# Turning denominators and normed tokens with DVE squares and DRAM transfers instead of TensorE transposes, in a two-layer attention kernel

## The chip, the cores and the metric

The kernel runs on one core of a Trainium2 chip, in 32-bit floating point. The metric is the device time of one execution in microseconds (us). Engine names are those of the profile: PE is TensorE's products, PEld its weight loads, DVE is VectorE, ACT is ScalarE, POOL is GpSimd, SP issues most transfers.

## The reference, cut to what matters

The input x has 4 batches of 128 channels and 4096 positions (64 x 64).

```python
# layer 0, per batch, with 64 inner channels m
q, k, v = wq @ xf, wk @ xf, wv @ xf                  # (64, 4096) each
att = softmax(k.T @ q, over j)                        # 4096 x 4096
x = x + wo @ (att @ v.T).T
# layer 1, on tokens t = x.T, 128 channels
t = t + causal_attention(layernorm(t), Wq, Wk, Wv)    # 4096 x 4096, scale 128 ** -0.5
# recurrent layer: Wx = layernorm(t) @ W.T, normalised over all tokens with gamma and beta
y_t = sigmoid(Wx_t + y_(t-1) @ V.T)
t = t + y
```

What must be seen for the change: both attentions end in a softmax whose denominators are sums over keys, and both are followed by a layernorm over the 128 channels of a token, whose result is used in two layouts, tokens on partitions and channels on partitions.

## The kernel before, in words

The fast path treats layer 0 of a batch, then layer 1 of the same batch, then the next batch; after the fourth batch comes the recurrent stage. Queries are taken in blocks g of 512 (8 per batch and layer). For each block the keys are passed in items; an item is a pair of key tiles of 128. In layer 0 a block has 16 items. Layer 1 is causal, so block g has 2g full items and two shorter ones on the diagonal: block 0 has 2 items, block 7 has 16.

One loop over all items, in slots, sets the order of the work. In slot s, `scores` (L656 in layer 0, L665 in layer 1) multiplies keys by the block's query rows into s_ps, and ACT takes the exponential into one of four buffers p (L670, L672). In layer 1 POOL clears what lies above the diagonal (L676). `sums` (L694 to L704) adds p into dsum on DVE. Two slots later `values` (L716, L724) multiplies p by the values and accumulates in acc. With the last item of a block, `values` copies acc out (L735 and L736, or L738) to agg, and DVE adds the two halves of dsum to den (L740), which has keys on partitions and the block's 512 queries along the row. The denominator of a query is therefore the sum of den over the partitions.

What follows a block is done in steps that are pushed into a list with a slot at which they fall due; at most one of them is taken per slot:

- `project` (L523 to L541): PE turns den in four 128x128 transposes into den_ps (L528), DVE sums each row of it (L530) and takes the reciprocal (L531). PE multiplies agg by the output weights into o_ps (L534), and DVE scales by the reciprocals and adds to xs, which holds the residual by tokens (L539).
- `normed` (L543 to L557): DVE takes mean and variance of each token (L548, L549), POOL the power -0.5 (L436), DVE one step of refinement (L437 to L440) and the normed tokens xh (L555).
- `transposed` (L559 to L564): PE turns the four 128x128 tiles of xh into a PSUM tile, and ACT (layer 0, xhT_ps) or DVE (layer 1, xh2T_ps) copies it to xhT.

In layer 0 (`finish0`) projection and norm fall due two slots after the block's last values; the transposes wait in the list `fill` for the end of the next block. In layer 1 (`finish1`) there are three steps, 1, 3 and 1 slots apart: projection, norm and the store of the tokens to x2 in DRAM; the transposes; the product with W into wx_ps (L609), its statistics (L612), and a copy to xs that reorders columns by time step (L614).

`rows` prepares the query rows of the block after the next. In layer 1 it is a product with xhT (L519) and a copy on DVE (L521); in layer 0 it also issues the load of the tokens of in_xT over xs (L512), on SP's queue. While layer 1 of a batch runs, `side` holds the key and value products of the next batch (L476, L488, L498), whose swapped halves go through transfers (L482), on SP's queue too.

The framework (Tile) decides the final order of instructions within each engine, close to but not exactly the order of the program. The pools: `misc` PSUM tiles have two buffers for all of den_ps, o_ps, r_ps, wx_ps, kr_ps and v_ps; the work pool has two buffers per name.

Of the kernel before, what the change touches and what calls it, by code (L numbers as in the profile page):

```python
# [9 lines left out]
F32 = mybir.dt.float32  # L10
AF = mybir.ActivationFunctionType
ALU = mybir.AluOpType
AX = mybir.AxisListType
PSUM = bass.MemoryType.PSUM

P = 128
BLK = 512
# [332 lines left out]
def fast_path(  # L350
# [21 lines left out]
    nc = tc.nc  # L372
    B, C, N = x.shape
    M = c_wqT.shape[1]
    assert C == P and M == P // 2 and N % CHUNK == 0
    NT = N // P
    NB = N // BLK
    TPB = BLK // P
    SHIFT = 32.0
    LOW, HIGH = 1e-25, 1e25  # L380
    WARM, TOL, STEPS = 12, 1e-6, 16
    NCH = N // STEPS
    CPB = BLK // STEPS

    const = ctx.enter_context(tc.tile_pool(name="const", bufs=1))
    xpool = ctx.enter_context(tc.tile_pool(name="x", bufs=1))
    dram = ctx.enter_context(tc.tile_pool(name="dram", bufs=1, space=bass.MemoryType.DRAM))

    xs = xpool.tile([P, B, N], F32, name="xs")
# [27 lines left out]
    ident = const.tile([P, P], F32, name="ident")  # L419
# [6 lines left out]
    nc.gpsimd.memset(mhalf, -0.5)  # L426
    minus = const.tile([P, P], F32, name="minus")
    nc.vector.tensor_scalar(minus, ident, -1.0, None, ALU.mult)
    good = const.tile([P, 1], F32, name="good")
    g1 = const.tile([P, P], F32, name="g1")  # L430
    recs = const.tile([P, 2, B, NT], F32, name="recs")
# [10 lines left out]
    with tc.tile_pool(name="batch", bufs=1) as batch, tc.tile_pool(name="rows", bufs=2) as rowp, tc.tile_pool(  # L442
        name="prob", bufs=4
    ) as prob, tc.tile_pool(name="work", bufs=2) as wk, tc.tile_pool(name="stat", bufs=4) as stat, tc.tile_pool(
        name="ps_s", bufs=2, space=PSUM
    ) as ps_s, tc.tile_pool(name="ps_a", bufs=1, space=PSUM) as ps_a, tc.tile_pool(
        name="ps_m", bufs=2, space=PSUM
    ) as ps_m:

        def misc(name):  # L450
            return ps_m.tile([P, BLK], F32, tag="m", name=name)
# [8 lines left out]
        bs = [Batch() for _ in range(B)]  # L460
# [60 lines left out]
            nc.vector.tensor_copy(r, ps)  # L521
            bs[b].next.append(r)

        def project(layer, b, g, agg, den):

            dp = misc("den_ps")
            for j in range(TPB):
                nc.tensor.transpose(dp[:, ts(j, P)], den[:, ts(j, P)], ident)  # L528
            rec = recs[:, layer, b, ts(g, TPB)]
            nc.vector.tensor_reduce(rec, dp.rearrange("p (j k) -> p j k", k=P), AX.X, ALU.add)  # L530
            nc.vector.reciprocal(rec, rec)  # L531
            op = misc("o_ps")
            for j in range(TPB):
                nc.tensor.matmul(  # L534
                    op[:, ts(j, P)], lhsT=agg[:, ts(j, P)], rhs=wv1 if layer else wo2, start=True, stop=True
                )
            for j in range(TPB):
                t = xs[:, b, ds(g * BLK + j * P, P)]
                nc.vector.scalar_tensor_tensor(  # L539
                    t, in0=op[:, ts(j, P)], scalar=rec[:, j : j + 1], in1=t, op0=ALU.mult, op1=ALU.add  # L540
                )  # L541

        def normed(b, g, dst):  # L543

            st = stat.tile([P, TPB, nc.vector.BN_STATS_DIM], F32, tag="st", name="ln_st")
            mv = stat.tile([P, TPB, nc.vector.BN_AGGR_DIM], F32, tag="mv", name="ln_mv")
            for j in range(TPB):
                nc.vector.bn_stats(st[:, j], xs[:, b, ds(g * BLK + j * P, P)])  # L548
                nc.vector.bn_aggr(mv[:, j], st[:, j])  # L549
            var = stat.tile([P, TPB], F32, tag="var", name="ln_var")  # L550
            nc.vector.tensor_scalar(var, mv[:, :, 1], LN_EPS, None, ALU.add)  # L551
            y = stat.tile([P, TPB], F32, tag="rstd", name="ln_rstd")
            rsqrt(y, var, stat.tile([P, TPB], F32, tag="z", name="ln_z"))
            for j in range(TPB):
                nc.vector.tensor_scalar(  # L555
                    dst[:, j], xs[:, b, ds(g * BLK + j * P, P)], mv[:, j, 0:1], y[:, j : j + 1], ALU.subtract, ALU.mult
                )  # L557

        def transposed(src, dst, name, engine):  # L559

            ps = misc(name)
            for j in range(TPB):
                nc.tensor.transpose(ps[:, ts(j, P)], src[:, j], ident)
            engine(dst, ps)  # L564

        def in_range():

            r = recs.rearrange("p l b t -> p (l b t)")
            r2 = stat.tile([P, 2 * B * NT], F32, tag="r2", name="r2")
            nc.vector.tensor_scalar(r2, r, LOW, None, ALU.is_ge)  # L570
            nc.vector.tensor_scalar(r, r, HIGH, None, ALU.is_le)
            nc.vector.tensor_tensor(r, r, r2, ALU.mult)
            nc.vector.tensor_reduce(good, r, AX.X, ALU.add)

        def finish0(b, g):

            agg, den = bs[b].agg, bs[b].den

            def norm():
                if g == 0:  # L580
                    bs[b].xh = batch.tile([P, NT, P], F32, tag="xh", name="xh")
                    bs[b].xhT = batch.tile([P, N], F32, tag="xhT", name="xhT")
                normed(b, g, bs[b].xh[:, ts(g, TPB)])

            yield 2, lambda: (project(0, b, g, agg, den), norm())
            fill.append(
                lambda: transposed(bs[b].xh[:, ts(g, TPB)], bs[b].xhT[:, ts(g, BLK)], "xhT_ps", nc.scalar.copy)
            )

        def finish1(b, g):  # L590
            agg, den = bs[b].agg, bs[b].den
            mem = {}

            def first():
                project(1, b, g, agg, den)
                nc.sync.dma_start(
                    out=x2[b, ts(g, BLK)].rearrange("(j p) c -> p j c", p=P),
                    in_=xs[:, b, ts(g, BLK)].rearrange("p (j c) -> p j c", c=P),
                )
                mem["xh"] = wk.tile([P, TPB, P], F32, tag="xh2", name="xh2")  # L600
                normed(b, g, mem["xh"])

            def second():
                mem["xhT"] = wk.tile([P, BLK], F32, tag="xhT2", name="xhT2")
                transposed(mem["xh"], mem["xhT"], "xh2T_ps", nc.vector.tensor_copy)

            def third():
                wp = misc("wx_ps")
                nc.tensor.matmul(wp, lhsT=wf, rhs=mem["xhT"], start=True, stop=True)  # L609
                if b == B - 1 and g == NB - 1:  # L610
                    in_range()
                nc.vector.bn_stats(stats[:, b * NB + g], wp)  # L612

                nc.scalar.copy(  # L614
                    xs[:, b, ts(g, BLK)].rearrange("p (s c) -> p s c", c=CPB),
                    wp.rearrange("p (c s) -> p s c", s=STEPS),
                )

            yield 1, first
            yield 3, second  # L620
            yield 1, third


        class Item:
# [118 lines left out]
        fill = []  # L743

        def push(slot, chain):
            step = next(chain, None)
            if step:
                waiting.append((slot + step[0], step[1], chain))

        def keys(b, m):  # L750
            mem = []
            return [
                lambda: cols0(b, m),
                lambda: mem.append(vals0(b, m)),
                lambda: vals0_by_tokens(b, m, mem[0]),
            ]
# [17 lines left out]
        for s in range(len(items) + SKEW + 16):  # L774
            if s < len(items):
                it = items[s]
                if it.first:
                    bs[it.b].rows = bs[it.b].next.pop(0)
                    if it.layer and it.g == 1 and it.b + 1 < B:
                        for m in range(NB // 2):  # L780
                            side += keys(it.b + 1, m)
                scores(it)
            if 0 <= s - SKEW < len(items):
                it = items[s - SKEW]
                values(it)
                if it.last:
                    rows()
                    if fill:
                        fill.pop(0)()
                    push(s, (finish1 if it.layer else finish0)(it.b, it.g))  # L790
            if s < len(items):
                sums(items[s])
            due = [w for w in waiting if w[0] <= s]
            if due:
                w = min(due, key=lambda w: w[0])
                waiting.remove(w)
                w[1]()
                push(s, w[2])
            elif side:
                side.pop(0)()  # L800
# [7 lines left out]
    with tc.tile_pool(name="xr", bufs=1) as xrp, tc.tile_pool(name="y", bufs=2) as yp, tc.tile_pool(  # L808
        name="ps_y", bufs=1, space=PSUM
# [19 lines left out]

        by_step = xs.rearrange("p b (g s c) -> p b s g c", s=STEPS, c=CPB)  # L830
        start = xrp.tile([P, B, NCH + 1], F32, name="start")
        nc.gpsimd.memset(start[:, :, 0:1], 0.0)
        prev = [None] * B
        grid = lambda t: t.rearrange("p (g c) -> p g c", c=CPB)
        pair = lambda t: t.rearrange("p (h q) -> p h q", q=P)
# [51 lines left out]
        for b in range(B):  # L887
# [3 lines left out]
            sq = yp.tile([P, NCH], F32, tag=f"y{b}", name="sq")  # L891
# [70 lines left out]
```

## Time and profile before

| | |
|---|---|
| time, median of 14 runs | 2163.92 us (2162.0 to 2165.71) |
| profiled execution, its own time | 2164.8 us |
| its span in the profile | 2163.1 us |
| PE busy | 2115.7 us, 98% |
| DVE busy | 1434.9 us, 66% |
| ACT busy | 1008.0 us, 47% |
| transposes of den (L528), in 256 instructions | 40.1 us busy |
| transposes of xh, layer 0 and layer 1 (L563), 128 instructions each | 20.4 and 21.4 us busy |
| DVE reduction of den_ps (L530), 64 | 43.7 us, 683 ns each |
| DVE copy of xh2T_ps and ACT copy of xhT_ps (L564), 32 each | 21.9 and 19.0 us |
| transfers: swap, x2 store, in_xT load, us from issue to landing | 2.2, 2.3, 3.3 |

Busy time is the time in which at least one instruction of the engine runs. Instructions on PE overlap, and their ends are modelled, so what one group costs PE is better read from the distance between the starts of neighbours in the order of time than from its busy time or the mean of one. Semaphore instructions don't count as busy.

### The profile page before, as it was taken

Reading aid. Unit: us, or ns where it says so; the run is one execution under the profiler, and the core shown is the slowest. Engines: PE = TensorE matmul, PEld = TensorE weight load, DVE = VectorE, ACT = ScalarE, POOL = GpSimd, SP = SyncE. Lnnn points to the kernel's source line nnn. Section 1 sums busy time; section 2 is a strip of 40 time slices with the busy share of each in tenths; the row PEclk is TensorE's granted clock in tenths of the full one; section 3 lists DMA queues with packets and bytes.
Section 4 is the critical chain, followed back from the end, with each engine's and each line's share of the span. In section 5 each row is a group of like instructions: output and inputs, shape, how many; then the busy total and the mean of one; then the engine's idle time right before and its main releaser. Section 6 shows DMA issues by size and latency. Waiting matters only on the chain. (4 is left out here: it accounts for less than half of the span.)

```text
span 2163.1 us, 30424 instructions
## 1 busy us (share of the span) xinstructions
PE 2115.7 (98%) x12204; PEld 941.8 (44%) x12204; DVE 1434.9 (66%) x2703; ACT 1008.0 (47%) x1098; POOL 104.5 (5%) x207
## 2 busy tenths in 40 slices
PE   6999999999999999999999999999999999999978
PEld 2333354444333344444333335444433334544446
DVE  3888865444788876554588886544478887654468
ACT  4666633323566643323466663323356664332355
POOL 0000010000000010000000001000000001000000
PEclk9999999999999999999999999999999999999989
DMA  7000011000000001100000001100000000000043
GB/s 224 2 1 2 1 30 49 5 6 5 6 2 1 1 20 30 35 5 5 6 1 1 1 1 30 49 5 5 5 6 2 1 2 6 10 10 5 5 161 157
DMA packets 42997, 48.72 MB, mean 23 GB/s; under 512 B 3168, under 2 KB 36704, under 8 KB 40800
## 3 DMA queue, kind: packets, MB, share of 16 engines
q1 hardware_dynamic: 40960, 46.15, 6.5%
q8 instruction: 97, 1.59, 0.3%
q10 hardware_dynamic: 1888, 0.56, 0.1%
q14 instruction: 52, 0.43, 0.1%
HBM read 25.72 MB, written 16.78 MB: 20 GB/s over the span
## 5 line engine op out<-in xcount | busy, mean ns | idle before, releaser
L696 DVE TENSOR_TENSOR dsum<-dsum,p 128x1024 f32<-128x1024 f32 x676 | 827.9, 1225 | 465.0 <-ACT p L672 335.5
L670 ACT ACTIVATE p<-s_ps,nshift 128x1024 f32<-128x1024 f32 x512 | 571.3, 1116 | 359.8 <-PE s_ps L656 340.3
L672 ACT ACTIVATE p<-s_ps 128x1024 f32<-128x1024 f32 (+2 forms) x288 | 274.2, 952 | 598.8 <-PE s_ps L665 496.2
L716 PE MATMUL acc<-p,v 64*64 64x512 f32 x4096 | 533.2, 591 | 1.7 <-ACT half L735 1.7
L656 PE MATMUL s_ps<-swap,kr 64*64 64x512 f32 x2048 | 530.1, 595 | 1.0 <-DMA swap<-kr 1.0
L656 PE MATMUL s_ps<-kr 64*64 64x512 f32 x2048 | 530.1, 595 | 0.0
L665 PE MATMUL s_ps<-rows,xhT 128*128 128x512 f32 (+3 forms) x1152 | 503.9, 559 | 0.0
L724 PE MATMUL acc<-p,xh 128*128 128x512 f32 (+3 forms) x1152 | 501.5, 557 | 0.0
L724 PEld LDWEIGHTS acc<-p,xh 128*128 128x128 f32 x1152 | 215.6, 190 | 241.3 <-issue 231.8
L665 PEld LDWEIGHTS s_ps<-rows,xhT 128*128 128x128 f32 x1152 | 211.0, 190 | 227.1 <-issue 189.7
L716 PEld LDWEIGHTS acc<-p,v 64*64 64x64 f32 x4096 | 155.3, 133 | 285.1 <-issue 266.1
L656 PEld LDWEIGHTS s_ps<-swap,kr 64*64 64x64 f32 x2048 | 137.4, 133 | 132.5 <-issue 124.2
L656 PEld LDWEIGHTS s_ps<-kr 64*64 64x64 f32 x2048 | 137.4, 133 | 128.3 <-issue 123.7
L436 POOL TENSOR_TENSOR ln_rstd<-ln_var,mhalf 128x4 f32<-128x4 f32 x64 | 66.1, 1032 | 1219.2 <-DVE ln_var L551 1219.2
L704 DVE TENSOR_TENSOR dsum<-dsum,p 128x256 f32<-128x256 f32 (+1 forms) x120 | 55.9, 499 | 72.0 <-POOL p L676 72.0
L694 DVE COPY dsum<-p 128x1024 f32<-128x1024 f32 x60 | 41.4, 690 | 68.5 <-ACT p L672 57.2
L539 DVE SCALAR_TENSOR_TENSOR xs<-o_ps,recs,xs 128x128 f32<-128x128 f32 x256 | 73.0, 344 | 8.9 <-PE o_ps L534 2.8
L555 DVE TENSOR_SCALAR xh<-xs,ln_mv,ln_rstd 128x128 f32<-128x128 f32 x256 | 71.3, 342 | 2.2
L676 POOL TENSOR_SCALAR_AFFINE_SELECT p<-p 128x128 f32<-128x128 f32 x128 | 34.4, 292 | 672.7 <-ACT p L672 672.7
L548 DVE BATCH_NORM_STATS2 ln_st<-xs 128x6 f32<-128x128 f32 x256 | 63.5, 269 | 0.0
L861 DVE SCALAR_TENSOR_TENSOR z<-xs,scale,y_ps 128x256 f32<-128x256 f32 x108 | 48.6, 480 | 6.6 <-PE y_ps L859 5.4
L614 ACT COPY xs<-wx_ps 128x512 f32<-128x512 f32 x32 | 18.7, 584 | 73.0 <-DVE stats L612 73.0
(104 smaller groups left out, 1056.2 us busy)
## 6 DMA issues: line engine op xcount, KB each, us to landing
xs<-in_x SPq DMA_DIRECT2D x16, 512.0 KB, 7.3
xs<-in_xT SPq DMA_DIRECT2D x32, 256.0 KB, 3.3
x<-xs SPq DMA_DIRECT2D x32, 256.0 KB, 2.3
xr<-x SPq DMA_DIRECT2D x8, 1024.0 KB, 12.0
out_x<-xr SPq DMA_DIRECT2D x8, 1024.0 KB, 4.5
swap<-kr SPq DMA_DIRECT2D x32, 128.0 KB, 2.2
wo<-in_c_woT ACTq DMA_DIRECT2D x2, 32.0 KB, 4.3
wqT<-in_a_wqT ACTq DMA_DIRECT2D x1, 64.0 KB, 5.7
```

The source lines that it names most:

```text
L436: nc.gpsimd.tensor_tensor(y, var, mhalf[:, : y.shape[-1]], ALU.pow)
L539: nc.vector.scalar_tensor_tensor(t, in0=op[:, ts(j, P)], scalar=rec[:, j : j + 1], in1=t, op0=ALU.mult, op1=ALU.add)
L548: nc.vector.bn_stats(st[:, j], xs[:, b, ds(g * BLK + j * P, P)])
L555: nc.vector.tensor_scalar(dst[:, j], xs[:, b, ds(g * BLK + j * P, P)], mv[:, j, 0:1], y[:, j : j + 1], ALU.subtract, ALU.mult)
L656: nc.tensor.matmul(ps[c * M : c * M + M, off : off + n], lhsT=bs[it.b].kr[part, h, ds(t % (NT // 2) * P + c * M, M)], rhs=rows[h], start=True,
L665: nc.tensor.matmul(ps[:, off : off + n], lhsT=lhsT, rhs=rhs, start=True, stop=True)
L670: nc.scalar.activation(it.p[:, :off], ps[:, :off], AF.Exp, bias=nshift)
L672: nc.scalar.activation(it.p[:, :off], ps[:, :off], AF.Exp, scale=float(P) ** -0.5)
L696: nc.vector.tensor_tensor(flat, flat, it.p, ALU.add)
L704: nc.vector.tensor_tensor(den[:, h, q0:], den[:, h, q0:], it.p[:, o : o + n], ALU.add)
L716: nc.tensor.matmul(bt.acc[h * M : h * M + M, r], lhsT=bt.v[part, t], rhs=it.p[part, o : o + n], start=it.first, stop=it.last,)
L724: nc.tensor.matmul(bt.acc[:, 0, q0:], lhsT=bt.xh[:, t], rhs=it.p[:, o : o + n], start=it.first and h == 0, stop=it.last and h == 1,)
```

## The change

Both layers stop turning den and xh on PE (but for the last block of all).

*Denominators.* DVE transposes den in 32x32 squares (`folded`): the instruction exchanges rows and columns within each square, so the 512 columns become 16 squares side by side on four groups of 32 partitions. Summing each square's 32 columns leaves 16 partial sums per partition. PE adds the four partition groups with one product of 16 columns by a constant `fold` (a 128x128 matrix of 32x32 identities); DVE multiplies by the constant `quarter`, which keeps for each partition the column of its own group, and sums over four.

*Normed tokens.* DVE transposes xh in 32x32 squares (`squares`); the squares are then in place inside but stand on the wrong partition group. In layer 1 four transfers write them to a DRAM tile and one reads xhT back, in an order of columns in which a group's queries are interleaved (the copy L614 undoes it). In layer 0 four transfers write in pieces of 128 bytes and four read rows of 2 KB. All are on SP's queue.

*Order.* In layer 0, one slot after a block's end den is folded, and the projection is put into `fill` and so comes at the end of the next block; the norm follows one slot later, squares and transfers two later. In layer 1 the third step comes four slots after the second instead of one, but for the last block. A small buffer of the range check is taken from den's buffers.

```diff
+    dram2 = ctx.enter_context(tc.tile_pool(name="dram2", bufs=2, space=bass.MemoryType.DRAM))
...
+    fold = const.tile([P, P], F32, name="fold")
+    nc.vector.tensor_reduce(
+        fold[:, :S], ident.rearrange("p (q r) -> p r q", r=S), AX.X, ALU.add
+    )
+    for q in range(1, Q):
+        nc.vector.tensor_copy(fold[:, ts(q, S)], fold[:, :S])
+
+    quarter = const.tile([P, TPB, Q], F32, name="quarter")
+    for j in range(TPB):
+        nc.vector.tensor_reduce(quarter[:, j], ident.rearrange("p (q r) -> p q r", r=S), AX.X, ALU.add)
...
-        def project(layer, b, g, agg, den):
+        def folded(den):
+
+            sq = wk.tile([P, TPB * Q, S], F32, tag="sq", name="sq")
+            nc.vector.transpose(out=sq.rearrange("p a b -> p (a b)"), in_=den)
+            part = stat.tile([P, TPB * Q], F32, tag="part", name="part")
+            nc.vector.tensor_reduce(part, sq, AX.X, ALU.add)
+            return part
+
+        def project(layer, b, g, agg, part):
 
             dp = misc("den_ps")
-            for j in range(TPB):
-                nc.tensor.transpose(dp[:, ts(j, P)], den[:, ts(j, P)], ident)
             rec = recs[:, layer, b, ts(g, TPB)]
-            nc.vector.tensor_reduce(rec, dp.rearrange("p (j k) -> p j k", k=P), AX.X, ALU.add)
+
+
+            nc.tensor.matmul(dp[:, : TPB * Q], lhsT=fold, rhs=part, start=True, stop=True)
+            own = stat.tile([P, TPB, Q], F32, tag="own", name="own")
+            nc.vector.tensor_tensor(own, dp[:, : TPB * Q].rearrange("p (j q) -> p j q", q=Q), quarter, ALU.mult)
+            nc.vector.tensor_reduce(rec, own, AX.X, ALU.add)
             nc.vector.reciprocal(rec, rec)
...
+        def squares(src):
+
+            sq = wk.tile([P, Q, TPB, S], F32, tag="sqT", name="sqT")
+            nc.vector.transpose(out=sq.rearrange("p c j t -> p j c t"), in_=src.rearrange("p j (c r) -> p j c r", r=S))
+            return sq
...
-            yield 2, lambda: (project(0, b, g, agg, den), norm())
-            fill.append(
-                lambda: transposed(bs[b].xh[:, ts(g, TPB)], bs[b].xhT[:, ts(g, BLK)], "xhT_ps", nc.scalar.copy)
-            )
+            def by_channels():
+                sq = squares(bs[b].xh[:, ts(g, TPB)])
+                by_r = dram2.tile([S, Q, TPB, Q, S], F32, tag="by_r", name="by_r")
+                for q in range(Q):
+                    nc.sync.dma_start(
+                        out=by_r[:, :, :, q].rearrange("r c j t -> r (c j) t"),
+                        in_=sq[ts(q, S)].rearrange("r c j t -> r (c j) t"),
+                    )
+                for c in range(Q):
+                    nc.sync.dma_start(
+                        out=bs[b].xhT[ts(c, S), ts(g, BLK)], in_=by_r[:, c].rearrange("r j q t -> r (j q t)")
+                    )
+
+            def rest():
+                yield 1, norm
+                yield 2, by_channels
+
+            def first():
+                part = folded(den)
+
+                def second(s):
+                    project(0, b, g, agg, part)
+                    push(s, rest())
+
+                fill.append(second)
+
+            yield 1, first
...
             def first():
-                project(1, b, g, agg, den)
+                project(1, b, g, agg, folded(den))
...
             def second():
                 mem["xhT"] = wk.tile([P, BLK], F32, tag="xhT2", name="xhT2")
-                transposed(mem["xh"], mem["xhT"], "xh2T_ps", nc.vector.tensor_copy)
+                if final:
+                    transposed(mem["xh"], mem["xhT"], "xh2T_ps", nc.vector.tensor_copy)
+                    return
+
+
+                sq = squares(mem["xh"])
+                by_c = dram2.tile([Q, S, Q, P], F32, tag="by_c", name="by_c")
+                for q in range(Q):
+                    nc.sync.dma_start(
+                        out=by_c[:, :, q].rearrange("c r k -> r c k"),
+                        in_=sq[ts(q, S)].rearrange("r c j t -> r c (j t)"),
+                    )
+                nc.sync.dma_start(out=mem["xhT"], in_=by_c.rearrange("c r q k -> (c r) (q k)"))
...
-                nc.scalar.copy(
-                    xs[:, b, ts(g, BLK)].rearrange("p (s c) -> p s c", c=CPB),
-                    wp.rearrange("p (c s) -> p s c", s=STEPS),
-                )
+                to = xs[:, b, ts(g, BLK)]
+                if final:
+                    nc.scalar.copy(to.rearrange("p (s c) -> p s c", c=CPB), wp.rearrange("p (c s) -> p s c", s=STEPS))
+                else:
+                    nc.scalar.copy(
+                        to.rearrange("p (s j q u) -> p s j q u", q=Q, j=TPB, s=STEPS),
+                        wp.rearrange("p (q j u s) -> p s j q u", q=Q, j=TPB, s=STEPS),
+                    )
 
             yield 1, first
             yield 3, second
-            yield 1, third
+            yield 1 if final else 4, third
...
                 if it.last:
                     rows()
                     if fill:
-                        fill.pop(0)()
+                        fill.pop(0)(s)
```

More of the change, by code (lines that the diff above doesn't have):

```diff
@@ L383, in fast_path @@
     CPB = BLK // STEPS
+    S = nc.vector.STREAM_SQUARE_SIZE
+    Q = P // S
     const = ctx.enter_context(tc.tile_pool(name="const", bufs=1))
@@ L564, in transposed @@
             engine(dst, ps)
+        def squares(src):
+            sq = wk.tile([P, Q, TPB, S], F32, tag="sqT", name="sqT")
+            nc.vector.transpose(out=sq.rearrange("p c j t -> p j c t"), in_=src.rearrange("p j (c r) -> p j c r", r=S))
+            return sq
         def in_range():
             r = recs.rearrange("p l b t -> p (l b t)")
-            r2 = stat.tile([P, 2 * B * NT], F32, tag="r2", name="r2")
+            r2 = wk.tile([P, BLK], F32, tag="den", name="r2")[:, : 2 * B * NT]
             nc.vector.tensor_scalar(r2, r, LOW, None, ALU.is_ge)
@@ L592, in finish1 @@
             mem = {}
+            final = b == B - 1 and g == NB - 1
             def first():
-                project(1, b, g, agg, den)
+                project(1, b, g, agg, folded(den))
                 nc.sync.dma_start(
```

## The prediction

> **What bounds the kernel now.** I read the page's busy times first, then the windows of single blocks, then the order of time on PE and DVE inside such a block.
>
> ```profile
> PE 2115.7 (98%) x12204; PEld 941.8 (44%) x12204; DVE 1434.9 (66%) x2703; ACT 1008.0 (47%) x1098; POOL 104.5 (5%) x207
> ```
>
> PE carries the end; over the whole span DVE looks free for a third of it. But that share is a mean over two layers. The windows of one block of layer 0 (16 slots; successive blocks start 29.86 us apart) and of a stretch of layer 1 tell them apart:
>
> ```profile
> core 0: us, PE busy (x) PEld busy (x) DVE busy (x) ACT busy (x) POOL busy (x), PEclk, DMA share, GB/s
> 1160.64:1190.50 29.86, 29.86 (x276) 11.37 (x272) 24.98 (x42) 19.20 (x19) 1.01 (x1) 1.00 0.01 2
> 420.00:450.00 30.00, 30.00 (x86) 14.83 (x85) 15.39 (x34) 8.59 (x10) 2.08 (x5) 1.00 0.03 10
> ```
>
> In layer 0 DVE is busy 25 of 29.9 us, in layer 1 half the time. How much of the last 4.9 us is really free? DVE in order of time at a block's end:
>
> ```profile
> 1191.63 13.21 DVE L696 TENSOR_TENSOR dsum<-dsum,p 128x1024 f32<-128x1024 f32 x10
> 1205.33 1.23 DVE L696 TENSOR_TENSOR dsum<-dsum,p 128x1024 f32<-128x1024 f32 x1 [0.49 <-ACT p L670]
> ...
> 1208.76 1.23 DVE L696 TENSOR_TENSOR dsum<-dsum,p 128x1024 f32<-128x1024 f32 x1 [0.88 <-ACT p L670]
> ...
> 1211.23 1.23 DVE L696 TENSOR_TENSOR dsum<-dsum,p 128x1024 f32<-128x1024 f32 x1 [0.64 <-ACT p L670]
> 1212.95 1.23 DVE L696 TENSOR_TENSOR dsum<-dsum,p 128x1024 f32<-128x1024 f32 x1 [0.49 <-ACT p L670]
> ...
> 1218.65 0.16 DVE L437 TENSOR_TENSOR ln_z<-ln_rstd 128x4 f32<-128x4 f32 x1 [1.12 <-POOL ln_rstd L436]
> ```
>
> Ten sums in a row take 13.21 us, so they follow each other every 1.33 us although each is busy 1.225: about 0.1 us of each is semaphore handling. The four idles that wait for p hold 2.50 us; taking 0.1 us of handling off each leaves **2.1 us really free per block**. The 1.12 us behind POOL's power is not free[...]. So DVE needs 29.86 - 2.1 = 27.75 us of a layer 0 block, and PE 29.86.
>
> What PE would give up, in order of time, layer 1 (the two transposes of the denominators and of the normed tokens):
>
> ```profile
> 304.97 0.60 PE L528 MATMUL den_ps<-ident,den 128*128 128x128 f32 x4
> 305.41 1.06 PE L534 MATMUL o_ps<-wv,agg 128*128 128x128 f32 x8
> 306.30 1.88 PE L665 MATMUL s_ps<-rows,xhT 128*128 128x512 f32 x4
> ...
> 317.90 0.60 PE L563 MATMUL xh2T_ps<-ident,xh 128*128 128x128 f32 x4
> 318.34 1.88 PE L665 MATMUL s_ps<-rows,xhT 128*128 128x512 f32 x4
> ```
>
> Start to start, four transposes hold PE 0.44 us. In layer 0, between 64-row products, they hold it longer: at 93.50 the next product starts at 94.09, and 0.1 us is lost ahead of it (0.69); the denominators' four about 0.5.
>
> [...] The trace has no DVE transpose; its other 512-element passes at that rate take 0.68 to 0.69 us (L530, L736, L740), so I price one at 0.69. [...] the trace agrees (swap 2.2, x<-xs 2.3 us to landing). [...]
>
> **The change part by part.** *PE, removed:* layer 1, 0.44 + 0.44 us per block; layer 0, 0.5 + 0.69. *Added:* the 16-column product. It loads weights as the o_ps products do (0.89 us for four, 0.22 each) and streams less: 0.2 us, between 0.1 and 0.25. Net 0.68 us in layer 1, 1.0 to 1.2 in layer 0 (PE would need about 28.7 there). Over 32 + 31 blocks (the last keeps its transposes): 37 + 21 = 58 us if nothing else binds.
>
> *DVE, layer 0, per block:* the square of den after it (0.12 because its start waits for den's end, 0.69, 0.05 handling) and its reduction (0.61 to the next start): +1.47. The reduction of den_ps goes (-0.72 with handling); the product with quarter and the small reduction come (0.21 each, as the 4-element rows): -0.29 together. The square of xh: +0.75. It also waits on five semaphores (four transfers and DVE), and one extra semaphore instruction costs about 0.07 between the sums: +0.26. Sum +2.2, so DVE needs 27.75 + 2.2 = **29.9 us, as much as a block takes now**. PE's 28.7 then don't count. The four p buffers carry PE over DVE's bursts, but not a deficit that repeats each block; already now ACT waits for DVE once a block:
>
> ```profile
> ACT p L670 <- DVE ln_st L548: 2.4, 4, 0.6
> ```
>
> (four blocks' waits). So layer 0 pays 0.07 us more in some 31 blocks: +2 us, where PE alone would save 37.
>
> *Layer 0, moved:* the projection waits one block longer (fill), and norm and transfers follow. The last block's set then falls into layer 1's block 1, the one before into block 0. Those blocks are short on PE (4 and 11 us of products plus the next batch's keys), and DVE is dense there. Adding up DVE's list from the end of layer 0 through block 1 with the durations of its rows gives 50 us, PE's 52 with two stalls of about 2 us (a rows copy and a misc buffer that DVE frees later); before, PE took 54.4 including transposes. Call it 0, from -2 to +3 per batch. Block 7's set falls into the next layer 0 and is hidden or lost with it.
>
> *Layer 1, blocks 2 to 6 or 7:* DVE gains the square of den and its reduction (+1.4) and exchanges the copy of xh2T_ps (0.68) for a square (0.69), but is half idle. The product waits for den, square and reduction (2.1 us after the last sum), and PE reaches it two items later, 6.9 us: covered. Net 0.68 x 5 or 6 x 4 = **-13.6 to -16 us**.
>
> *Transfers.* Layer 0: four writes of 512 pieces of 128 B, four reads of 32 x 2 KB per block. Two issues wait on SP for their landing. Their first reader, layer 1's block with the same number, is several blocks away; the worst, block 7, still has six blocks: nothing. Layer 1: four writes and one read, about 0.7 (square) + 2.3 + 2.5 + queueing 0.5 = 6 us; the third step is now four slots later, 13.8 us in full slots, 15 us of PE work in blocks 0 and 1. Ahead of it in SP's queue stand loads in_xT that wait for PE's value products, the swaps and the store x<-xs. In the changed kernel's compiled order of instructions the value product of block 0 is 15 us of PE work ahead of its wx; for block 1 the layer 0 transfers of block 7 lie ahead (its by_r split by a store that waits for DVE), about 18 of 25 us. Cost 0, cover 7 us; uncovered, PE would stand at wx_ps. Writes of 128 B are not in the trace[...].
>
> *ACT* loses the 0.60 us copy in layer 0 and has a finer output pattern in L614 (0.58 us); it has 10 us free per block: 0. *Tail:* the last projection waits for square and reduction (+1.4) and saves 0.24: +1. *Start:* the two constants fall into DVE's wait for the first loads: 0.
>
> Sum: +2 + 0 - 15 + 1 = -12 us. The profiled execution took 2164.8 us (span 2163.1 and 1.7 around it), 0.9 above the median of 2163.92; the sum against it gives 2152.8, near 2152 on the median. I take **2152**.
>
> **The rivals.**
> *A, DVE has room:* if POOL's wait is filled by other work (-1.1) or squares overlap their neighbours, DVE needs under 28.8 and PE stays the bound: -58 us, 2106; half of it 2130. For: 66% busy. Against: the four free idles are only 2.1 us, and in the compiled order ln_z follows ln_var directly.
> *B, slower: a 4-byte square takes longer than a plain pass.* Each 0.1 us more costs 0.2 x 32 in layer 0 and about 2 in the dense blocks: 8.4 us. From 0.83 us on the gain is gone[...]. Nothing in the trace excludes it.
> *C, the way through DRAM is late:* PE stands at wx_ps in 31 blocks; 2 us each would be +62 on -12, 2214. It decides from 7 us beyond my chain. Against: cover above.
> That the transposes stay is excluded: the compiled order has 64 small products and only the last block's transposes.
>
> **How the numbers follow.** About 0.2% (4.3 us) is what a measurement of this kernel can tell from no change. Main case 0.45, own range 2142 to 2162 (0.35 faster, 0.08 same, 0.02 slower); A 0.2 (faster); B 0.25 (0.03 same, 0.22 slower); C 0.1 (0.02 same, 0.08 slower). That makes 0.55, 0.13, 0.32. For 8 in 10 the range reaches from half of A down (2116) to most of B (2184).
>
> **What would show it.** Right: layer 0 blocks still about 29.9 us apart, DVE without waits for p there, ACT waiting for DVE or PE's products late; layer 1 blocks 2 to 6 shorter by 0.7; a square at 0.69 us; no PE idle ahead of wx_ps. Wrong: layer 0 blocks at 28.7 (A), squares over 0.8 (B), PE waiting on xhT's transfer (C).

## The result, and the profile after

| | median, us | lowest to highest | ratio to before, 95% interval |
|---|---|---|---|
| before | 2163.47 (28 runs) | 2161.91 to 2165.71 | |
| changed kernel | 2138.88 (6 runs) | 2136.99 to 2143.33 | 0.9888 [0.9878, 0.9898] |

The change makes the kernel 24.6 us faster. The forecast was 12 us. Its wide range, 2116 to 2184, holds the result; the main case's own range, 2142 to 2162, does not. The sign and the main mechanism were right; the sum was wrong by a factor of two, about half of it in the layer 0 term and half in layer 1 and the end. The profiled execution spans 2136.6 us, 26.5 less than before.

The page's first line of busy times of the changed kernel:

```profile
PE 2075.8 (97%) x11824; PEld 911.2 (43%) x11824; DVE 1521.2 (71%) x2935; ACT 991.6 (46%) x1066; POOL 103.0 (5%) x207
```

And the windows of one steady block of layer 0 (from one addition into den to the next) and of the same stretch of layer 1 as before:

```profile
core 0: us, PE busy (x) PEld busy (x) DVE busy (x) ACT busy (x) POOL busy (x), PEclk, DMA share, GB/s
713.70:743.17 29.47, 29.17 (x274) 10.78 (x270) 26.62 (x45) 18.76 (x17) 1.01 (x1) 1.00 0.09 19
420.00:450.00 30.00, 30.00 (x85) 14.72 (x84) 18.38 (x41) 9.64 (x11) 2.08 (x5) 1.00 0.07 18
```

PE still looks full (97%), but in the layer 0 block it is no longer: 29.17 of 29.47 us. The block takes 29.47 us instead of 29.86. Who sets that is read from DVE in order of time:

```profile
713.70 0.69 DVE L811 TENSOR_TENSOR den<-dsum 128x512 f32<-128x512 f32 x1
714.43 0.71 DVE L541 STREAM_TRANSPOSE sq<-den 128x512 f32<-128x512 f32 x1
715.17 0.69 DVE L543 TENSOR_REDUCE part<-sq 128x16 f32<-128x512 f32 x1
715.78 0.68 DVE L765 COPY dsum<-p 128x1024 f32<-128x1024 f32 x1
716.57 1.23 DVE L767 TENSOR_TENSOR dsum<-dsum,p 128x1024 f32<-128x1024 f32 x1
717.71 0.17 DVE L554 TENSOR_TENSOR own<-den_ps,quarter 128x16 f32<-128x16 f32 x1
717.91 0.17 DVE L555 TENSOR_REDUCE recs<-own 128x4 f32<-128x16 f32 x1
718.11 0.18 DVE L556 RECIPROCAL recs<-recs 128x4 f32<-128x4 f32 x1
718.21 0.66 DVE L807 TENSOR_TENSOR agg<-half 128x512 f32<-128x512 f32 x1
718.79 1.12 DVE L564 SCALAR_TENSOR_TENSOR xs<-o_ps,recs,xs 128x128 f32<-128x128 f32 x4
...
723.42 0.17 DVE L451 TENSOR_TENSOR ln_z<-ln_rstd 128x4 f32<-128x4 f32 x1 [1.12 <-POOL ln_rstd L450]
...
724.22 1.12 DVE L580 TENSOR_SCALAR xh<-xs,ln_mv,ln_rstd 128x128 f32<-128x128 f32 x4
725.37 0.71 DVE L594 STREAM_TRANSPOSE sqT<-xh 128x512 f32<-128x512 f32 x1
726.01 17.13 DVE L767 TENSOR_TENSOR dsum<-dsum,p 128x1024 f32<-128x1024 f32 x13
743.17 0.69 DVE L811 TENSOR_TENSOR den<-dsum 128x512 f32<-128x512 f32 x1
```

From 713.70 to 743.17 DVE waits for no p at all; its one idle is POOL's 1.12 us. Before, four waits for p stood here. So DVE binds this block, as forecast; the experiments below test it. And between 640 and 735 us ACT now waits for DVE to free p, 8.5 us in little more than three blocks, where before it was 2.4 in four:

```profile
ACT p L741 <- DVE dsum L767: 8.5, 11, 2.2
```

Where the time went, from the starts of the first exponential of each block, after minus before, summed over the four batches (us):

| stretch | sum | by batch |
|---|---|---|
| layer 0, block 0 | -5.0 | -0.45, -0.18, -1.79, -2.54 |
| layer 0, block 1 | -6.6 | -1.64 each |
| layer 0, blocks 2 to 6 | -10.0 | -2.1 to -2.8 |
| layer 0, block 7 | +10.4 | +1.80, +3.44, +1.81, +3.38 |
| layer 1 | -14.1 | -3.7, -3.7, -3.7, -3.0 |
| start and end | -1.3 | |

Block 1 has no projection any more, since the first block's has moved one block later, and block 7 and layer 1's first blocks get it back. Blocks 0, 1 and 7 together make -1.1. But for rounding, the parts add up to the difference of the spans, 26.5. The real gain of layer 0 is in blocks 2 to 6: block 2 takes 28.94 us, block 3 some 29.15, blocks 4 to 6 mostly 29.47. I read this as PE running ahead of DVE until the four p buffers are used up, and following DVE from then on.

### The profile page after: what moved, and what is told of

Same layout as the page of the kernel before. It is cut to its first block, busy times and chain, and to the rows that moved or that the text cites. A ratio compares the mean times of both kernels' runs of the same rounds, so it can differ in the third digit from the quotient of the medians.

```text
span 2136.6 us, 30557 instructions
## 1 busy us (share of the span) xinstructions
PE 2075.8 (97%) x11824; PEld 911.2 (43%) x11824; DVE 1521.2 (71%) x2935; ACT 991.6 (46%) x1066; POOL 103.0 (5%) x207
## 3 DMA queue, kind: packets, MB, share of 16 engines
q1 hardware_dynamic: 137008, 79.20, 13.6%
q8 instruction: 95, 1.56, 0.3%
## 5 line engine op out<-in xcount | busy, mean ns | idle before, releaser
L787 PE MATMUL acc<-p,v 64*64 64x512 f32 x4096 | 574.2, 592 | 1.7 <-ACT half L806 1.7
L727 PE MATMUL s_ps<-kr 64*64 64x512 f32 x2048 | 571.1, 594 | 4.7 <-ACT p L741 4.7
L787 PEld LDWEIGHTS acc<-p,v 64*64 64x64 f32 x4096 | 169.4, 133 | 282.7 <-issue 274.9
L727 PEld LDWEIGHTS s_ps<-kr 64*64 64x64 f32 x2048 | 153.3, 133 | 144.5 <-issue 124.1
```

Source lines behind the costliest of these rows:

```text
L727: nc.tensor.matmul(ps[c * M : c * M + M, off : off + n], lhsT=bs[it.b].kr[part, h, ds(t % (NT // 2) * P + c * M, M)], rhs=rows[h], start=True,
L787: nc.tensor.matmul(bt.acc[h * M : h * M + M, r], lhsT=bt.v[part, t], rhs=it.p[part, o : o + n], start=it.first, stop=it.last,)
```

## The experiments

Times are medians, and "faster than the changed kernel" is the difference of two medians. The kernel before, measured beside each group of runs, had medians from 2162.6 to 2164.0 us, so about 1 us of such a difference can come from the group.

**The two layers, each alone.** Layer 0's steps taken back to those of before, and then layer 1's:

```diff
 # layer 1 alone: finish0 as before
-            yield 1, first
+            yield 2, lambda: (project(0, b, g, agg, None, den), norm())
+            fill.append(
+                lambda s: transposed(bs[b].xh[:, ts(g, TPB)], bs[b].xhT[:, ts(g, BLK)], "xhT_ps", nc.scalar.copy)
+            )
 # layer 0 alone: finish1 as before
-                project(1, b, g, agg, folded(den))
+                project(1, b, g, agg, None, den)
-                if final:
+                if True:
                     transposed(mem["xh"], mem["xhT"], "xh2T_ps", nc.vector.tensor_copy)
-            yield 1 if final else 4, third
+            yield 1, third
```

> Layer 1 of the changed kernel with layer 0 as before (PE transposes of den and xh there). If layer 1 pays what its blocks lose on PE (0.68 us in each of blocks 2 to 7, and 14.1 us summed over the four batches in the comparison of traces), this kernel is 12 to 16 us faster than before. If the gain of layer 1 is really made by layer 0's work having left its first blocks or by PE running ahead in layer 0, it is under 6 us here.

> Layer 0 of the changed kernel with layer 1 as before. Main theory: layer 0 is bound by DVE at 29.47 us a block against 29.86 of PE before, 0.39 us less in 32 blocks: 8 to 13 us faster than before. Rival 1, as forecast (DVE needs 29.93): 0 to 3 us slower, and the gain sits elsewhere. Rival 2, PE binds layer 0 and its time fell by 1.6 us in each block, part of it being lost again in layer 1: over 20 us faster.

Layer 1 alone: 2143.95 us, 0.9908 [0.9892, 0.9925], 19.6 us faster, above what I expected. Its trace has 16.3 us in layer 1 (4.1 per batch, blocks 5 to 7 at -0.59, -0.71 and -0.66) and the start, the end and layer 0 differ by +0.7, -1.6 and -0.4 us. Layer 0 alone: 2158.60 us, 0.9978 [0.9969, 0.9986], 5.0 us faster, below what I expected from 0.39 x 32: in its trace blocks 2 to 6 give 10 us as in the changed kernel, but blocks 0, 1 and 7 together take 3.5 of it back, and the profiled execution (2156.55 us) was one of its fastest. The two parts add up to the whole, 19.6 + 5.0 = 24.6, closer than their intervals promise. The forecast had -14 (layer 1 and the end) and +2: it missed by 5.6 and 7.

**One more square for DVE in layer 0.**

```diff
                 part = folded(den)
+                extra = wk.tile([P, BLK], F32, tag="sq", name="sq_twice")
+                nc.vector.transpose(out=extra, in_=den)
```

> The changed kernel with den turned once more in each layer 0 block into a tile that nobody reads. Main theory (DVE binds layer 0 in all but the first blocks of a batch, and what PE runs ahead there is given back at the end): each block pays the whole 0.74 us from start to start, 32 x 0.74 = 24 us slower than the changed kernel (20 to 25), back to before. Rival, PE or waits on transfers bind layer 0: under 8 us slower.

2151.95 us, 0.9948 [0.9931, 0.9964]: 13.1 us slower than the changed kernel, between the two expectations. The steady blocks tell why. Their period is 29.91 us, 0.44 more and not 0.74, and DVE in order of time shows that the square itself cost no more:

```profile
719.37 0.71 DVE L541 STREAM_TRANSPOSE sq<-den 128x512 f32<-128x512 f32 x1
720.00 0.67 DVE L636 STREAM_TRANSPOSE sq_twice<-den 128x512 f32<-128x512 f32 x1
720.60 0.64 DVE L543 TENSOR_REDUCE part<-sq 128x16 f32<-128x512 f32 x1
721.16 0.68 DVE L767 COPY dsum<-p 128x1024 f32<-128x1024 f32 x1
```

From sq to part it takes 1.23 us instead of 0.74, and from part to the copy 0.56 instead of 0.61: 0.44 in sum. Part needs sq's result and starts 0.74 after it; with an independent instruction between the two, each follows in 0.60 to 0.63. So the extra square filled a wait that was already there. 0.44 in 32 blocks is 14.1 us, against 13.1 measured: DVE binds layer 0, and my price for the square, all of its 0.74, was wrong.

**Relief for DVE: no first copy.** The second item's sum adds the first two p, and the copy of the first into dsum goes, in layer 0 alone.

```diff
-                if it.first:
-                    nc.vector.tensor_copy(flat, it.p)
+                if it.first and it.layer == 0:
+                    bs[it.b].p0 = it.p
+                elif it.first:
+                    nc.vector.tensor_copy(flat, it.p)
+                elif bs[it.b].p0 is not None:
+                    nc.vector.tensor_tensor(flat, bs[it.b].p0, it.p, ALU.add)
+                    bs[it.b].p0 = None
```

> The changed kernel without the copy that begins a block's sum in layer 0: the second item's sum adds the first two p and writes dsum. DVE loses 0.79 us (start to start) in each layer 0 block and PE and ACT lose nothing. Main theory: layer 0 blocks fall to 28.7 us, 20 to 25 us faster than the changed kernel, 45 to 50 faster than before. Rival, PE or transfers bind layer 0: under 6 us faster than the changed kernel.

2122.09 us, 0.9810 [0.9793, 0.9826], 16.8 us faster than the changed kernel. Again DVE binds, and again the sum was off: the blocks fall from 29.47 to 28.94, not to 28.7. The denominators' products of two successive blocks, in PE's order of time:

```profile
651.28 0.39 PE L553 MATMUL den_ps<-part,fold 128*128 128x16 f32 x2
...
680.22 0.40 PE L553 MATMUL den_ps<-part,fold 128*128 128x16 f32 x2
```

All blocks from 2 to 6 have 28.94, and block 7 loses 0.25 us instead of 1.8 to 3.4. In a window of one such block PE is busy without a gap (28.94 of 28.94): here PE binds again. So 28.94 is what PE needs. That block 7's loss in the changed kernel was DVE's lag being made up is my reading of it: nearly all of the loss goes with the copy.

**The same relief for the kernel before.** No first copy, and the norm of layer 0 cut in two steps, one slot apart, meant to let sums stand in DVE's wait for POOL (`tail` holds the refinement and the four products into xh):

```diff
-            rsqrt(y, var, stat.tile([P, TPB], F32, tag="z", name="ln_z"))
+            nc.gpsimd.tensor_tensor(y, var, mhalf[:, :TPB], ALU.pow)
...
+            late.append(tail)
...
             yield 2, lambda: (project(0, b, g, agg, den), norm())
+            yield 1, lambda: late.pop()()
```

> The kernel before with DVE relieved in layer 0: no first copy (0.79 us a block) and the norm cut in two steps, one slot apart, so that a sum of p can stand in DVE's wait for POOL (1.12 us). Main theory: before, PE binds layer 0 at 29.86 us a block and DVE's relief is worth nothing: within 3 us of before. If DVE bound the kernel before as well, it would be over 15 us faster, as the same relief made the changed kernel (16.8 us for the copy alone).

2163.04 us, 0.9994 [0.9986, 1.0003]: nothing, and the blocks stay where they were:

```profile
670.28 0.66 PE L529 MATMUL den_ps<-ident,den 128*128 128x128 f32 x4
700.13 0.66 PE L529 MATMUL den_ps<-ident,den 128*128 128x128 f32 x4
```

The cut did not do what it was meant to. In DVE's order of time ln_z still follows ln_var, and the wait for POOL stands in 28 of the 32 blocks of layer 0:

```profile
675.12 0.17 DVE L552 TENSOR_SCALAR ln_var<-ln_mv 128x4 f32<-128x4 f32 x1
676.41 0.17 DVE L562 TENSOR_TENSOR ln_z<-ln_rstd 128x4 f32<-128x4 f32 x1 [1.12 <-POOL ln_rstd L558]
```

What this run tests is therefore the copy alone, and that is enough: the bound of layer 0 went from PE (29.86) to DVE (29.47), and a DVE saving that is worth 16.8 us after the change is worth nothing before it.

**The two edits of layer 0 apart.** First den by PE again, at the place of the fold product, with xh's squares kept; then den's squares kept, with xh turned by PE again, in two placements.

```diff
 # xh's squares alone
-                part = folded(den)
-                    project(0, b, g, agg, part)
+                    project(0, b, g, agg, None, den)
 # den's squares alone: two slots after the norm, and seven
-                yield 2, by_channels
+                yield 2, lambda: transposed(bs[b].xh[:, ts(g, TPB)], bs[b].xhT[:, ts(g, BLK)], "xhT_ps", nc.scalar.copy)
+                yield 7, lambda: transposed(bs[b].xh[:, ts(g, TPB)], bs[b].xhT[:, ts(g, BLK)], "xhT_ps", nc.scalar.copy)
```

> The changed kernel, but in layer 0 den is turned by PE again, at the place where the changed kernel has its fold product; xh goes by squares and transfers. DVE then needs 27.75 + 0.75 = 28.5 us a block and PE, which loses only the xh transposes, 28.94 + about 0.3 = 29.2. Main theory: layer 0 blocks at 29.2 instead of 29.47, PE bound: 2 to 8 us faster than the changed kernel. If the five waits of sqT and its transfers cost DVE time that the traces don't show, or if den's squares were free, it is as fast as the changed kernel or slower.

> The changed kernel, but in layer 0 PE turns xh again (two slots after the norm) and ACT copies it; den goes by squares. If the experiments before are read rightly, den's squares free only 0.17 us of PE a block (28.94 with both edits and DVE relieved, 29.11 with xh's squares alone), and DVE needs 28.7: PE binds layer 0 at about 29.7 us a block, 0.2 more than the changed kernel. With layer 1 and without the waits for the transfers at a batch's end: 2136 to 2146 us. If den's squares free 0.3 us of PE as forecast, blocks stand at 29.55 and the time at 2134.

> As the kernel with den's squares alone in layer 0, but PE's transposes of xh come seven slots after the norm instead of two, so that they don't wait for xh and don't set off the half clock that followed 20 such waits there. If den's squares free 0.17 us of PE a block, as the steady blocks of 28.94 and 29.11 us say, layer 0 blocks stand at 29.7 us, and the kernel at 2136 to 2146 us. If they free 0.3 us as forecast, 29.55 us and some 2133. If the 102 us of the first version came from anything but those waits and the half clock after them, it stays over 2160.

Xh's squares alone: 2126.18 us, 0.9823 [0.9806, 0.9839], 12.7 us faster than with both edits. The period is right (29.1), the gain larger than expected, because block 7 loses only 0.44 us here:

```profile
679.71 0.66 PE L554 MATMUL den_ps<-ident,den 128*128 128x128 f32 x4
708.82 0.66 PE L554 MATMUL den_ps<-ident,den 128*128 128x128 f32 x4
```

Den's squares alone, late: 2147.65 us, 0.9930 [0.9912, 0.9948], just above my bracket, with the period that I expected, 29.69:

```profile
658.51 0.40 PE L552 MATMUL den_ps<-part,fold 128*128 128x16 f32 x2
...
688.20 0.40 PE L552 MATMUL den_ps<-part,fold 128*128 128x16 f32 x2
```

In both kernels PE is busy without a gap over such a block (29.11 of 29.11, 29.69 of 29.69), so these are PE's periods. This settles the two edits in PE's account: xh's squares free 29.86 - 29.11 = 0.75 us of PE a block, den's 29.86 - 29.69 = 0.17, and both 0.92 = 29.86 - 28.94. On DVE the traces give den's squares as +0.98 (below) and xh's as +0.76. In layer 0, den's squares are a bad bargain: 0.98 us of the engine that becomes the bound for 0.17 us of the other.

The early placement was a miss of mine: 2240.75 us, 1.0358 [1.0341, 1.0375]. PE met the transposes before xh was ready, once a block. PE in order of time, and three windows around it:

```profile
1195.31 1.04 PE L787 MATMUL acc<-p,v 64*64 64x512 f32 x8
1198.83 1.09 PE L588 MATMUL xhT_ps<-ident,xh 128*128 128x128 f32 x4 [2.48 <-DVE xh L580]
1199.85 1.12 PE L727 MATMUL s_ps<-swap,kr 64*64 64x512 f32 x2
...
1203.30 0.59 PE L727 MATMUL s_ps<-swap,kr 64*64 64x512 f32 x2
```

```profile
1196.00:1198.00 2.00, 0.35 (x4) 0.00 (x0) 0.80 (x5) 0.67 (x1) 1.01 (x1) 1.00 0.00 0
1200.00:1202.00 2.00, 2.00 (x12) 0.65 (x16) 1.90 (x2) 0.64 (x2) 0.00 (x0) 0.50 0.03 8
1204.00:1206.00 2.00, 2.00 (x24) 0.70 (x20) 0.73 (x2) 1.12 (x1) 0.00 (x0) 1.00 0.00 0
```

The figure after the engines' busy times is PEclk, the granted clock: after an idle of 2.48 us it falls to 0.50, and the same products take 1.12 us instead of 0.59. The trace has 20 such stretches in layer 0, five in each batch, each 3.41 us long, and a mean granted clock of 0.979, against 0.993 with the transposes five slots later; by my estimate one stretch costs up to half of its 3.41 us, 1.7 us. Idle and half clock make 4.2 of the 4.7 us by which these blocks exceed 29.69. Moving the transposes five slots later took 93 us off.

**The waits for DRAM at a batch's end.** The changed kernel's waits of PE have a row that the one before has not:

```profile
PE wx_ps L676 <- DMA xhT<-by_c: 5.9, 3, 2.0
```

```diff
-            yield 1 if final else 4, third
+            yield 1 if final else 7 if g == NB - 1 else 4, third
```

> The changed kernel with the product into wx_ps seven slots after the squares instead of four for the last layer 1 block of each of the first three batches, whose slots lie in layer 0 and are half as long. The trace shows PE waiting there for the read back from DRAM three times, 5.9 us in all. Main theory (the three waits are on the path, and nothing takes their place): 4 to 7 us faster than the changed kernel. Rival (layer 0 of the next batch is bound by DVE, PE has that time to spare): under 2 us.

2134.15 us, 0.9860 [0.9844, 0.9877], 4.7 us faster than the changed kernel. The row is gone from the waits, so the three waits were on the path. (In the traces the first blocks of the next batches are 6.3 us shorter; a half clock stretch behind one of the waits goes with it, but one more than before stands in the block 7s; the mean granted clock is 0.992 in both.) They stand at the last layer 1 block of a batch, and 13.8 us for four slots, my cover, held for full slots of layer 1; these slots lie in layer 0, where one takes 29.5 / 16 = 1.84 us.

**All three together:** no first copy, the cut norm, the later product.

> The changed kernel with all three: no first copy in layer 0, the norm of layer 0 cut in two steps one slot apart, and the later product into wx_ps. Main theory: with the copy gone DVE needs 28.7 us and PE binds layer 0 at 28.94, so the cut norm adds nothing there and only the 5.9 us of the three waits are to be had beside the copy's 16.8: 2112 to 2119 us. If DVE's wait for POOL still cost time, blocks would fall further below 28.9 and the time below 2110.

2116.51 us, 0.9777 [0.9761, 0.9793]: 47 us faster than before, 22.4 faster than the changed kernel, and the best version here. Its blocks of layer 0 stand at 28.94 and it has no half clock before the recurrent stage (mean granted clock 0.994, against 0.992 in the changed kernel). That is the copy's 16.8 and the 4.7 of the waits; 0.9 is left, no more than the groups of runs can differ by. The cut norm tells nothing here either: DVE's wait of 1.12 us for POOL again stands in 28 of 32 blocks, so whether DVE time beyond the copy would still be worth something was not tried.

**Layer 1: its room on DVE, and its two edits.** An extra square of den in layer 1, and den turned by PE again in layer 1:

```diff
 # extra square
                 project(1, b, g, agg, folded(den))
+                extra = wk.tile([P, BLK], F32, tag="sq", name="sq_twice")
+                nc.vector.transpose(out=extra, in_=den)
 # den by PE
-                project(1, b, g, agg, folded(den))
+                project(1, b, g, agg, None, den)
```

> The changed kernel with den turned once more in each layer 1 block into a tile that nobody reads. Main theory: DVE has room in layer 1, the 0.74 us lie beside PE in nearly all 32 blocks: within 4 us of the changed kernel. If DVE bound layer 1 too: 15 to 24 us slower.

> The changed kernel, but in layer 1 den is turned by PE again. It splits layer 1's gain (19.6 us when it was made alone) between the two edits. As forecast, a block of layer 1 loses 0.44 us of PE for xh and 0.24 for den: 0.24 in some 28 blocks, 5 to 8 us slower than the changed kernel. If den's squares are worth as little as in layer 0 (0.17 us), 4 to 5 us slower; if they lengthen the chain to the projection more than they free PE, no slower.

The extra square: 2147.90 us, 0.9930 [0.9913, 0.9946], 9.0 us slower than the changed kernel, more than I expected and less than a bound would make. In blocks 4 to 7 of layer 1 it costs nothing (the same time to 0.01 us); blocks 0 to 2, where DVE is dense, pay about 1 us per batch. The rest is spread over the ends of layer 0 (five half clock stretches ahead of the recurrent stage against three, mean granted clock 0.990 against 0.992) and the end. Den by PE: 2145.83 us, 0.9922 [0.9905, 0.9938], 7.0 us slower. Blocks 5 to 7 of layer 1 take 0.21 us more, which the changed kernel's PE shows too:

```profile
437.90 0.29 PE L552 MATMUL den_ps<-part,fold 128*128 128x16 f32 x2
438.05 1.14 PE L559 MATMUL o_ps<-wv,agg 128*128 128x128 f32 x8
439.02 1.88 PE L736 MATMUL s_ps<-rows,xhT 128*128 128x512 f32 x4
```

From den_ps to the next s_ps it is 1.12 us; before it was 1.33 (304.97 to 306.30). In the trace that makes 2.6 us of layer 1; three half clock stretches more than in the changed kernel (mean granted clock 0.989 against 0.992), by my estimate at up to 1.7 us each, can hold the rest. So I met the forecast of 5 to 8 us in part by chance.

## Why the prediction was right or wrong, point by point

**What binds layer 0: right.** DVE takes over from PE, as the forecast said against its rival A. The relief before and after the change, and the extra square, show it from three sides. Part of A's argument was right all the same: instructions did fill waits of others, so DVE's need fell below the forecast, but not under 28.8.

**DVE's need: the step that failed.** The forecast had 27.75 + 2.2 = 29.9 us a block (the 27.75 count DVE's wait of 1.12 us for POOL as needed, which was my estimate) and so +2 us for layer 0; DVE's need is 29.47. Term by term, from the changed kernel's order of time. First the lines of before that these terms are compared with:

```profile
1190.60 1.11 DVE L555 TENSOR_SCALAR xh<-xs,ln_mv,ln_rstd 128x128 f32<-128x128 f32 x4
...
1206.59 0.69 DVE L740 TENSOR_TENSOR den<-dsum 128x512 f32<-128x512 f32 x1
1207.20 0.69 DVE L694 COPY dsum<-p 128x1024 f32<-128x1024 f32 x1
...
1214.09 0.68 DVE L530 TENSOR_REDUCE recs<-den_ps 128x4 f32<-128x512 f32 x1
1214.81 0.18 DVE L531 RECIPROCAL recs<-recs 128x4 f32<-128x4 f32 x1
1215.08 1.13 DVE L539 SCALAR_TENSOR_TENSOR xs<-o_ps,recs,xs 128x128 f32<-128x128 f32 x4
```

- Square of den and reduction +1.47: from den to the copy 715.78 - 713.70 = 2.08 us, before 0.61. +1.47, right to the hundredth.
- Square of xh +0.75: from xh to the next sum 726.01 - 724.22 = 1.79, before 1.03 (1190.60 to 1191.63). +0.76, right.
- The exchange in the projection, -0.29 forecast: before, from the reduction of den_ps to xs 1215.08 - 1214.09 = 0.99; after, from own to xs 718.79 - 717.71 = 1.08, of which agg's addition takes 0.58. That leaves 0.50: **-0.49**. I had priced instructions and not the waits between dependent ones: from the reciprocal to the next start it was 0.27 us before and is 0.10 now, since agg's addition, which needs no result of it, stands there.
- The wait of sqT on five semaphores, +0.26 forecast: sqT starts 1.15 us after the group of four xh, which itself lasts 1.12. **0.** I had multiplied a cost that I took from the sums.

27.75 + 1.47 + 0.76 - 0.49 + 0 = 29.49, against 29.47 measured. That it closes to 0.02 is in part luck: agg's addition itself costs 0.58 from start to start, before 0.79, while one sum that took 1.14 takes 1.32 now and the refinement's steps take 0.80 instead of 0.67, and these cancel. With this the same argument gives 0.39 us less in each block instead of 0.07 more: about -12 in place of +2, of which the changed kernel shows 11.1, and layer 0 alone 5.0.

**PE's need: too low.** 28.7 forecast, 28.94 measured, since den's squares free 0.17 us and not 0.3; xh's free 0.75, a little more than the 0.69 forecast. (The forecast's own figures, 0.5 + 0.69 - 0.2, give 28.87; its 28.7 took the upper end of its 1.0 to 1.2.) It did not enter the sum, but rival A's 2106 rested on it: with DVE relieved, the kernel stands at 2116 to 2122.

**Layer 1: right in kind, at the upper end in size.** -13.6 to -16 forecast; 14.1 us in the trace of the changed kernel, 16.3 with layer 1 alone. Blocks 6 and 7 lose 0.71 and 0.66 us where 0.68 was forecast. The zone at the start of layer 1, forecast at 0 within -2 to +3 per batch, is not separable from it in the first three batches, because the next batch's products have moved among blocks 1 to 4. In the last batch, which has none, blocks 0 and 1 change by +1.56 and -1.55 us: 0, as forecast.

**The end: wrong by a little.** Forecast was +1, for den's square and reduction ahead of the last projection (in the last block only xh is still turned by PE). But the last o_ps also needs agg, and ACT's copy to agg began 3.88 us after the last exponential both before and after. Den's product was issued at 3.88 too, and o_ps at 4.51 in both. The chain was hidden: 0.

**Transfers (rival C): mostly as forecast.** From issue to landing they took 1.8 to 2.6 us (medians: by_r and by_c written in 2.2 and 1.8, read back in 2.0 and 2.6), near the 2.2 and 2.3 us of swap and x<-xs before. The forecast's 2.5 us for the read in layer 1 and 0.5 for queueing were my estimate. SP's queue did wait for the writes before it read back (us in total, times, longest):

```profile
SPq L625 <- DMA by_r<-sqT: 47.4, 28, 3.5
SPq L672 <- DMA by_c<-sqT: 34.0, 45, 2.7
```

In 28 of 31 blocks PE doesn't wait at wx_ps. The three at a batch's end were not costed, because the cover was worked out in layer 1's slots; they cost the changed kernel 4.7 us.

**Rival B: false.** A square takes 0.71 us in the rows above, 0.02 more than a plain pass. The upper end of the forecast's range, 2184, rested on this rival and was my estimate.

Forecast -12; its layer 0 term missed by 7 us and layer 1 with the end by 5.6, in the same direction. For the first the failed terms are shown. For the second, the trace of layer 1 alone has layer 1 at -16.3 where the sum had -15, and the end at -1.6 where it had +1. But the kernel with layer 0 alone, whose last blocks are as before, has -1.1 at the end too, so of the end no more than the missing +1 is shown. With the interval of layer 1 alone (16 to 23 us faster) I leave the rest open.

## What to carry to other kernels

When an edit moves work from a full engine to another, work out what the other needs in the stage in question, from start to start in the order of time: here the reduction started 0.74 us after the square it depends on, while with an independent instruction between the two each followed in 0.60 to 0.63, and such small terms made DVE's need 29.47 us where 29.9 was forecast. Then take the edits apart; here one gave 0.75 us of PE for 0.76 of DVE and the other 0.17 for 0.98, and only the first was worth having while DVE bound. With DVE relieved, den's 0.17 counts too, as the blocks of 28.94 against 29.11 us say. Count a distance in slots in the stage where those slots fall.

## What the runs showed of the hardware that I had not expected

- *PE's granted clock fell to half after some short waits.* In the kernel with the early transposes, after an idle of 2.48 us it was 0.50 for 3.41 us, so that by my estimate a wait of 2.5 us cost about 4.2. The changed kernel has three such stretches ahead of the recurrent stage: one just after a wait for DRAM of 1.91 us, two after waits of 1.60 and 1.61 us for DVE's copy of the query rows in layer 0's last block. The other two waits for that copy, 1.60 and 1.61 us, had none, and that is why this block takes now 1.8, now 3.4 us more; nor had the other two for DRAM, 1.99 and 1.98 us. So the length of the wait alone did not decide it. In the trace of the changed kernel the second and third stretch start 57 and 353 times 3.413 us after the first. What decides between waits of 1.60 to 1.99 us stays open.
- *An extra DVE instruction cost less than itself.* Between two dependent instructions a square of 0.67 us cost 0.44.
